# Reading two bands of the involution weights with one set of transfers, into two pair buffers of one tile

## The chip, the cores and the metric

The kernel runs on one core of one Trainium2 chip. The metric is the device time of one execution in microseconds; the median of three runs is the reference value. One further execution is taken with the hardware profiler, and every duration quoted below is from that one.

## What is computed

The input `x` is 32 images of 256 channels by 32 x 32 pixels in float32. Two layers follow each other, each with a group normalisation in front of it and a residual sum behind it. The first is a 3 x 3 convolution on values rounded to half precision, the second an involution: each pixel has its own 7 x 7 weights for each of 16 groups of channels, and these weights are made from the normalised image by two small matrix products.

```
x = x + conv3x3(quantize(gn(x))) + bias          # layer 0, 256 -> 256 channels
y = relu(bn(w1 @ gn(x)))                         # layer 1: 64 values for each pixel
w = w2 @ y + b2                                  # 16 groups x 49 taps for each pixel
out[g, c, h, w] = sum over 7x7 taps of w[g, tap, h, w] * gn(x)[g, c, h + dh, w + dw]
x = x + out
```

## The kernel before, in words

An image is cut in `K = 4` **bands** of 8 rows, and a band in a left and a right half of 16 columns. A half of a band is a **unit**: 8 units for each image (`M = 8`), 256 in all. Time is laid out by hand as **steps**, 16 for each image; the loop at the end walks through 570 steps and at each step issues, in this order, the next stage of up to four images' front, then the sums, the addition, the stores, the weights, the scatters, the loads of `x` and the loads of bands that are due. Every engine executes its own instructions in that order and waits on semaphores, which the recording layer derives from the tiles (named buffers) that an instruction reads and writes.

- **Front** (`front`, starting 56 steps ahead of an image's own first step): the statistics and the normalisation on ScalarE and VectorE, the convolution on TensorE (L332), the normalised image `xn`, the product `py` (L377) and `y_sb` (L388), and for each band the transposes `pt` (L396), which ScalarE copies into one of `NPIX = 6` `pixels` buffers (L400). The right half is stored mirrored (`backwards`).
- **Weights** (`weights`, 18 steps ahead, every second step): TensorE makes 4 rows of involution weights in `pw` (L411) and VectorE adds the bias and writes them into `w_sb`, a ring of `RING = 32` rows (`evict`, L435). `ring_pieces` cuts an eviction in pieces where the ring wraps.
- **Scatter** (`scatter`, L476): SyncE's queue issues seven transfers for each band that write `w_sb` into `wd`, a DRAM tensor in which every pixel holds its taps in the order in which they will be multiplied.
- **Band loads** (`load_bands`, L497, 9 steps ahead of a band's first step): for each of the 16 columns one transfer reads `wd` into a band buffer. There are `NBAND = 3` band buffers, each a tile of its own. A transfer has 8 rows by 2 halves, 16 runs of at most 4512 bytes. Two columns go to SyncE's queue, 14 to GpSimd's.
- **Sums** (`sums`, L522, one unit every second step): TensorE multiplies the `pixels` of the unit by its part of the band and accumulates in `acc`; one step later VectorE adds `acc` to the image in `x` (`add_windows`, L538), and `store` (L543) writes the image out in two halves.

Transfers issued on GpSimd's queue take eight completion semaphores in turn, so that each of them waits for the one that was issued eight before it.

Of the kernel before, what the change touches and what calls it, by code (L numbers as in the profile page):

```python
# [13 lines left out]
P = 128  # L14
# [22 lines left out]
XR = 4  # L37
# [22 lines left out]
TW = P // T  # L60
PAIR = 3 * GC
PAIRS = G // 2
ROW = S * WPIX
WR = 4
NBAND = 3
BY_SYNC = (0, 1)
ORDER = (0, 4, 8, 12, 2, 5, 9, 13, 3, 1, 6, 10, 14, 7, 11, 15)
NPIX = 6
RING = 32
SCRATCH = 4096  # L70
EARLY = CH + 4 + CH * CR
LATE = K1 * SW + 2 * 2 * SW
FRONT = -56
LOAD = -63
LEAD = 18


@with_exitstack
def tile_quant_conv_then_involution(
# [43 lines left out]
    x_tiles = {0: load_x(0)}  # L123


    ident = const.tile([P, P], F32, name="ident")
    make_identity(nc, ident)
    xq = const.tile([P, CH, H, W], F16, name="xq")
    eps = const.tile([P, 1], F32, name="eps")
# [13 lines left out]
    for t in bands[CH:]:  # L143
        nc.gpsimd.memset(t, 0.0)
    pixels = [const.tile([P, 2, PAIRS, PAIR], F32, name=f"pixels_{i}") for i in range(NPIX)]
    for t in pixels:
        nc.gpsimd.memset(t, 0.0)


    w_sb = const.tile([P, 2, RING, A, WIN, V], F32, name="w_sb")  # L150
    wd = dram.tile([H, S, WPIX], F32, name="wd")
    acc = [ps_acc.tile([P, RG, NT], F32, name=f"acc_{d}") for d in range(SIDES)]

    wq = const.tile([P, CH, K0 * K0, C], F16, name="wq")
    staged = []
    for kh in range(CH):
        wf = bands[kh].rearrange("p d n -> p (d n)")[:, : K0 * K0 * C].rearrange("p (k c) -> p k c", c=C)
# [21 lines left out]


    for col, cols, at, n in (
        (0, S, K1 * WB, PAD),
        (PAD1, PAD1, 0, PAD1 * WB),
        (W, PAD1, (K1 - PAD1) * WB, PAD1 * WB),
    ):
        to = bass.AP(
            tensor=wd.tensor,
            offset=wd.offset + col * WPIX + at,
            ap=[[ROW, H], [WPIX, cols], [1, n]],
        )  # L190
        nc.sync.dma_start(to, bands[NBAND - 1][:H, 0, :n].unsqueeze(1).to_broadcast([H, cols, n]))

    def quantize_weights(kh):

        nc.vector.tensor_scalar(wq[:, kh], staged[kh], F16_MAX, -F16_MAX, ALU.min, ALU.max)
        nc.gpsimd.memset(bands[kh], 0.0)
        if kh == CH - 1:
            nc.gpsimd.memset(w_sb, 0.0)

# [77 lines left out]
    def backwards(at):  # L277

        step, n = at.ap[-1]
        return bass.AP(tensor=at.tensor, offset=at.offset + step * (n - 1), ap=[*at.ap[:-1], [-step, n]])  # L280

    CONV = (9, 0, 9, 0)

    def front(b):
# [81 lines left out]
        for h in range(CH):  # L366
            yield
            to = xn[:, h].rearrange("p (k d r j) -> p d k r j", d=SIDES, r=TR, j=JC)
            at = xt[:, h].rearrange("p (k r d j) -> p d k r j", d=SIDES, r=TR, j=JC)
            gn.apply(h, [(to[:, 0], at[:, 0]), (to[:, 1], backwards(at[:, 1]))])  # L370
        yield from stages(2)

        py = ps_m.tile([P, NT], F32, tag="m", name="py")
# [10 lines left out]
        to = y_sb[b % 2].rearrange("p (k r d j) -> p d k r j", k=K, d=SIDES, j=JC)  # L384
        of = py.rearrange("p (k d r j) -> p d k r j", k=K, d=SIDES, j=JC)
        for d in range(SIDES):
            at = of[:, d]
            nc.scalar.activation(to[:, d], backwards(at) if d else at, AF.Relu, bias=bn_shift, scale=bn_scale)  # L388
        yield from stages(5)

        for m in range(0, M, 2):
            yield
            pt = ps_m.tile([P, 2, C], F32, tag="m", name="pt")
            for i in range(2):
                for h in range(CH):
                    nc.tensor.transpose(  # L396
                        pt[:, i, h * P : (h + 1) * P], xn[:, h, (m + i) * P : (m + i + 1) * P], ident
                    )
# [66 lines left out]
    def scatter(b, k, part):  # L465

        at = (b * H + k * TR) % RING
        for dj in range(part, K1, 2):
            t, e = divmod(dj, 2)
            to = bass.AP(  # L470
                tensor=wd.tensor,
                offset=wd.offset + k * TR * ROW + dj * WPIX + (K1 - 1 - dj) * WB,
                ap=[[WPIX, TW], [ROW, TR], [1, WB]],
            )
            rows = w_sb[t * TW : (t + 1) * TW, e, at : at + TR]
            nc.sync.dma_start(to, rows.rearrange("p s a r v -> p s (a r v)"))  # L476

    def load_bands(b, k):

        band = bands[(b * K + k) % NBAND]  # L480
        side = WINC * WB + PAD
        for i, j in enumerate(ORDER):
            cut = max(0, PAD1 - j)
            n = (K1 - cut) * WB + PAD
            src = bass.AP(
                tensor=wd.tensor,
                offset=wd.offset + k * TR * ROW + (j + PAD1) * WPIX + cut * WB,
                ap=[[ROW - V, TR], [(W - 1 - 2 * j) * WPIX - cut * WB, SIDES], [1, n]],
            )
            to = band[j::JC]  # L490
            to = bass.AP(
                tensor=to.tensor,
                offset=to.offset + (j + cut) * WB,
                ap=[to.ap[0], [side + (JC - 1 - 2 * j - cut) * WB, SIDES], [1, n]],
            )
            queue = nc.sync if j in BY_SYNC else nc.gpsimd
            queue.dma_start(to, src)  # L497

    def windows(b, m):
# [8 lines left out]
    def sums(b, m):  # L508

        k, d = divmod(m, SIDES)  # L510
        j0 = 0 if d else PAD1
        band = bands[(b * K + k) % NBAND][:, d]
        px = pixels[(b * K + k) % NPIX][:, d]
        for h in range(CH):
            for v in range(2):
                for g, at, top, f, l in windows(b, m):
                    p = slice(g * KP, (g + 1) * KP)
                    of = band[p, V * g * XR + j0 * WB : V * g * XR + (j0 + WINI) * WB]
                    of = of.rearrange("p (j a r v) -> p j a r v", a=A, r=WIN, v=V)
                    for t in range(T):  # L520
                        a = h * T + t
                        nc.tensor.matmul(  # L522
                            at[t * TW : (t + 1) * TW, h, :, f - top : l - top],
                            px[p, a, v * GC : v * GC + TW],
                            of[:, :, a, f - top : l - top, v],
                            start=(h, v) == (0, 0),
                            stop=(h, v) == (CH - 1, 1),
                        )
# [20 lines left out]
    def due(n, lag):  # L549

        b, i = divmod(n - lag, per)
        return (b, i) if 0 <= b < B else (None, None)

    with tc.manual_schedule():
        fronts = {}
        for n in range(FRONT, B * per + 2):
            b, i = due(n, FRONT)
            if i == 0:
                fronts[b] = front(b)
            later = list(fronts)  # L560
# [77 lines left out]
```

## Time and profile before

| what | value |
|---|---|
| runs | 1352.48 us median of 3 (1352.35 to 1356.02) |
| the profiled execution | 1344.24 us, of which 1342.5 us span |
| mean granted TensorE clock | 0.982 |
| TensorE busy | 1253.6 us, 93% of the span |
| GpSimd busy (band loads alone 980.3 us) | 1014.4 us, 76% |
| VectorE busy | 818.8 us, 61% |
| ScalarE busy | 733.3 us, 55% |
| DMA engines, mean busy share from 90 to 1200 us | 0.97 at 283 GB/s |
| band loads on GpSimd's queue | 1792, 549 ns each |
| band loads on SyncE's queue | 256 |
| scatters on SyncE's queue | 896, 160 KB each |

A page of the profile gives the busy time of each engine, the same in 40 slices of the span, the queues of the DMA engines, the chain of waits that ended last, and the costliest groups of instructions with what ended the idle time before them. PE is TensorE's matmul, PEld its weight load, DVE VectorE, ACT ScalarE, POOL GpSimd and SP SyncE; `L497` is line 497 of the kernel before. A row of the timeline has its start and its length in us, the engine, the line, what was written from what, how many, and in brackets the idle time ahead of it with what ended that. An average over the span mixes three stages: the start, in which only the front runs; a long steady stage; and the last three images, for which no front is left. A matmul of the kernel in float32 stands in the trace as two, so that a unit has 64 rows of L522 there.

### The profile page before, as it was taken

To read this page: it belongs to the slowest core of one execution; us is meant where nothing else is said; L and a number is where in the kernel's file an instruction comes from. 1 tells how busy PE (TensorE), PEld (TensorE's weight loads), DVE (VectorE), ACT (ScalarE), POOL (GpSimd) and SP (SyncE) were. 2 spreads that over 40 slices of the span, in tenths; PEclk is the share of its full clock that TensorE was granted. 3 is DMA by queue.
4 is the path that set the end of the run, shared out by engine and by line. 5 is a ranking of instruction groups with operands and counts; after the bars stand their busy time and mean duration, and the time that the engine had idled before them with its cause. 6 is when DMAs were issued, how large, how long until landed. Compare 5 with 4: busy or idle time off the path is not lost.

```text
span 1342.5 us, 65799 instructions
## 1 busy us (share of the span) xinstructions
PE 1253.6 (93%) x27648; PEld 763.7 (57%) x27648; DVE 818.8 (61%) x2539; ACT 733.3 (55%) x1731; POOL 1014.4 (76%) x1818
## 2 busy tenths in 40 slices
PE   5899999999999999999999999999999999999665
PEld 2356566565555655556655556666555566556454
DVE  3466666565666665656665666766666666666442
ACT  5775656455656556556545655655556564553300
POOL 9067878777787778777778787788777877788785
PEclk9999999999999999999999999999999999999987
DMA  6089999999999999999999999999999999999995
GB/s 228 11 237 295 271 293 293 279 266 281 272 286 282 291 285 270 283 263 280 293 282 283 270 288 282 293 297 296 281 288 275 277 284 290 271 281 266 278 274 166
DMA packets 360724, 361.85 MB, mean 270 GB/s; under 512 B 75056, under 2 KB 304752, under 8 KB 359152
## 3 DMA queue, kind: packets, MB, share of 16 engines
q1 hardware_dynamic: 278512, 229.38, 56.8%
q0 software_dynamic: 81920, 128.28, 33.9%
q8 instruction: 220, 3.60, 1.1%
q14 instruction: 72, 0.59, 0.1%
HBM read 176.60 MB, written 180.76 MB: 266 GB/s over the span
## 4 chain that ended last, share of the span: by engine, by line
PE 60%; DMA 23%; POOL 7%; issue 3%; ACT 3%; DVE 2%; SPq 1%; POOLq 0%; DVEq 0%; ACTq 0%
PE pc L332 25%; PE acc L522 19%; DMA band<-wd 17%; PE pw L411 11%; POOL band L497 7%; DMA wd<-w_sb 6%; PE pt L396 3%; PE py L377 3%; ACT junk L214 1%; SPq L476 1%; DVE w_sb L435 1%; DMA x<-in_x 1%; ACT xn L273 0%; SPq L497 0%; ACT xq L273 0%
## 5 line engine op out<-in xcount | busy, mean ns | idle before, releaser
L497 POOL DMA_DIRECT2D band<-wd x1792 | 980.3, 549 | 315.7 <-DMA band<-wd 182.0
L435 DVE TENSOR_TENSOR w_sb<-pw,late_sb 128x224 f32<-128x224 f32 (+7 forms) x1280 | 330.4, 322 | 419.5 <-PE pw L411 419.2
L332 PE MATMUL pc<-xq,wq 128*128 128x496 f16 (+3 forms) x2304 | 535.2, 379 | 20.3 <-ACT xq L273 18.3
L522 PE MATMUL acc<-band,pixels 64*32 64x190 f32 (+1 forms) x16384 | 426.6, 332 | 51.8 <-DMA band<-wd 42.7
L522 PEld LDWEIGHTS acc<-band,pixels 64*32 64x32 f32 x16384 | 304.7, 107 | 159.7 <-issue 81.1
L332 PEld LDWEIGHTS <-wq 128*128 128x128 f16 x2304 | 206.7, 98 | 316.1 <-issue 102.7
L411 PE MATMUL pw<-late_sb,y 64*32 64x224 f32 (+1 forms) x8192 | 288.9, 333 | 10.8 <-issue 9.4
L538 DVE TENSOR_TENSOR x<-acc,x 128x380 f32<-128x380 f32 (+1 forms) x512 | 262.0, 512 | 32.2 <-PE acc L522 23.2
L411 PEld LDWEIGHTS pw<-late_sb,y 64*32 64x32 f32 x8192 | 186.5, 106 | 38.1 <-issue 21.0
L400 ACT COPY pixels<-pt 128x512 f32<-128x512 f32 x128 | 73.7, 576 | 228.6 <-PE pt L396 228.6
L214 ACT ACTIVATE junk<-x 128x512 f16<-128x512 f32 (+1 forms) x192 | 146.4, 763 | 14.7 <-DVE x L348 12.2
L214 ACT ACTIVATE junk<-x,mean 128x1024 f16<-128x1024 f32 x128 | 147.1, 1149 | 4.3
L245 ACT ACTIVATE s<-back,eps 128x2 f32<-128x2 f32 x64 | 18.9, 296 | 178.6 <-DVE back L230 178.6
L346 DVE TENSOR_SCALAR q<-pc 128x512 f16<-128x512 f32 x128 | 87.2, 681 | 17.6 <-PE pc L332 17.6
L273 ACT ACTIVATE xn<-x,off,rstd 128x512 f32<-128x512 f32 x128 | 96.2, 800 | 0.0
L348 DVE SCALAR_TENSOR_TENSOR x<-q,early_sb,x 128x512 f32<-128x512 f16 x128 | 94.2, 736 | 0.3
L396 PEld LDWEIGHTS pt<-ident,xn 128*128 128x128 f32 x512 | 63.9, 142 | 26.3 <-issue 2.5
L396 PE MATMUL pt<-ident,xn 128*128 128x128 f32 x512 | 78.0, 275 | 0.1
L273 ACT ACTIVATE xq<-x,off,rstd 128x1024 f16<-128x1024 f32 x64 | 75.7, 1227 | 0.0
L235 ACT ACTIVATE mean<-back 128x2 f32<-128x2 f32 x64 | 12.6, 196 | 101.4 <-DVE back L230 101.4
L377 PE MATMUL py<-xn,early_sb 128*64 128x512 f32 x256 | 62.2, 606 | 0.9 <-ACT xn L273 0.9
L224 DVE STREAM_TRANSPOSE across<-sums 128x32 f32<-128x32 f32 x128 | 26.3, 205 | 33.6 <-ACT junk L214 32.4
(40 smaller groups left out, 369.3 us busy)
## 6 DMA issues: line engine op xcount, KB each, us to landing
wd<-w_sb SPq DMA_DIRECT2D x896, 160.0 KB
band<-wd POOLq DMA_DIRECT2D x1664, 70.5 KB, 4.6
x<-in_x SPq DMA_DIRECT2D x64, 512.0 KB
out<-x SPq DMA_DIRECT2D x64, 512.0 KB
band<-wd POOLq DMA_DIRECT2D x128, 60.5 KB, 4.6
band<-wd SPq DMA_DIRECT2D x128, 50.5 KB
band<-wd SPq DMA_DIRECT2D x128, 40.5 KB
band<-in_w SPq DMA_DIRECT2D x2, 1152.0 KB
```

Of the source, the lines that this page charges most:

```text
L214: nc.scalar.activation(junk[:, n0:n1], src[:, h, n0:n1], func, bias=bias, accum_out=self.sums[:, i : i + 1])
L273: nc.scalar.activation(dst, src, AF.Identity, bias=self.off[:, one], scale=self.rstd[:, one])
L332: nc.tensor.matmul(pc.rearrange("p (r c) -> p r c", c=W)[:, r0 - nt * RT : r1 - nt * RT, c0:c1], wq[:, kh, k, mh * P : (mh + 1) * P], xq[: ...
L346: nc.vector.tensor_scalar(q, pc, F16_MAX, -F16_MAX, ALU.min, ALU.max)
L348: nc.vector.scalar_tensor_tensor(xt[:, mh, cols], q, bias_sb[:, mh : mh + 1], xt[:, mh, cols], ALU.add, ALU.add)
L377: nc.tensor.matmul(py[i * CR : (i + 1) * CR], w1_sb[:, kh, :], px[:, :, i], start=kh == 0, stop=kh == CH - 1,)
L396: nc.tensor.transpose(pt[:, i, h * P : (h + 1) * P], xn[:, h, (m + i) * P : (m + i + 1) * P], ident)
L411: nc.tensor.matmul(pws[i][t * TW : (t + 1) * TW, : dj.stop - dj.start, r], y_sb[b % 2][half, (r0 // 2 + r) * W : (r0 // 2 + r + 1) * W], w ...
L435: nc.vector.tensor_tensor(to, of[:, :, d0:d1], bias[:, :, d0:d1], ALU.add)
L497: queue.dma_start(to, src)
L522: nc.tensor.matmul(at[t * TW : (t + 1) * TW, h, :, f - top : l - top], px[p, a, v * GC : v * GC + TW], of[:, :, a, f - top : l - top, v], ...
L538: nc.vector.tensor_tensor(x_at, of, x_at, ALU.add)
```

## The change

Bands 2q and 2q + 1 of an image become a **pair**, loaded together. `wd` is laid out so that the two bands of a pair lie beside each other along the columns (`SP = 2 * 32 + 6` columns, 8 rows for each of `K // BOTH = 2` pairs). A transfer of `load_bands` takes up to four halves of one column: 8 rows by 4 units, 32 runs. Ten columns (`d` is `None`) are read so, the six at the borders of the halves in two transfers of 16 runs each, one for the left halves and one for the right halves. A pair thus has 18 transfers on GpSimd's queue (`BY_GPSIMD`) and 4 on SyncE's (`BY_SYNC`).

The three band tiles are replaced by one tile `lot` of two `halves`, each of which holds a pair. In each half a hole between its second and third unit holds one of the `pixels` buffers; the hole of the first also holds the identity for the transposes. `NPIX` goes from 6 to 5, `RING` from 32 to 24, the scratch for descriptors from 4096 to 2048. The right half is no longer mirrored: `backwards` is gone. `LEAD` goes from 18 to 20, so weights and scatters come two steps earlier against the sums. The pixel copies of the third and fourth band of an image come 1 and 3 steps later (`HELD`). The band loads of a pair are issued 9 steps (GpSimd) and 8 steps (SyncE) ahead of its first sums; step 9 ahead comes right after the last sums that read the same half, and one step before the first sums of the pair in the other half.

```
-ROW = S * WPIX
+BOTH = 2
+SP = BOTH * W + 2 * PAD1
+ROW = SP * WPIX
+STEP = WINC * WB + PAD
+UNITS = BOTH * SIDES
+HALF = (UNITS - 1) * STEP + (JC + PAD1) * WB + PAD
+HOLE = (SIDES - 1) * STEP + JC * WB + PAD
+BY_SYNC = ((0, 0), (15, 1), (1, 0), (14, 1))
+BY_GPSIMD = (
+    (8, None), (4, None), (0, 1), (15, 0), (9, None), (5, None), (1, 1), (14, 0), (10, None),
+    (6, None), (2, 1), (13, 0), (11, None), (7, None), (2, 0), (13, 1), (12, None), (3, None),
+)
+NPIX = 5
+RING = 24
+SCRATCH = 2048
-NBAND = 3
-BY_SYNC = (0, 1)
-NPIX = 6
-RING = 32
-SCRATCH = 4096
-LEAD = 18
+LEAD = 20
+HELD = (0, 0, 1, 3)
...
+    lot = const.tile([P, 2 * HALF], F32, name="band_lot")
+    halves = [lot[:, i * HALF : (i + 1) * HALF] for i in range(2)]
+    holes = [t[:, HOLE : HOLE + 2 * PAD1 * WB] for t in halves]
+    ident = holes[0][:, 2 * PAIRS * PAIR :][:, :P]
...
-    bands = [const.tile([P, SIDES, WINC * WB + PAD], F32, name=f"band_{i}") for i in range(NBAND)]
...
-    wd = dram.tile([H, S, WPIX], F32, name="wd")
+    wd = dram.tile([K // BOTH, TR, SP, WPIX], F32, name="wd")
...
+            yield from stages(HELD[m // 2])
             to = pixels[(b * M + m) // 2 % NPIX].rearrange("p i a (v c) -> p (i a) v c", c=GC)
             nc.scalar.copy(to[:, :, ::2], pt.rearrange("p i (a v c) -> p (i a) v c", v=2, c=GC))
-            yield
+            yield from stages(1 - HELD[m // 2])
...
+    def load_bands(b, q, queue, columns):
+
+        for j, d in columns:
+            units, side, step = (UNITS, 0, 1) if d is None else (BOTH, d, SIDES)
+            cut = max(0, PAD1 - j) if d == 0 else 0
+            end = min(K1, JC + PAD1 - j) if d == 1 else K1
+            n = (end - cut) * WB + PAD
             src = bass.AP(
                 tensor=wd.tensor,
+                offset=wd.offset + (q * TR * SP + side * JC + j + PAD1) * WPIX + cut * WB,
+                ap=[[ROW - V, TR], [step * JC * WPIX, units], [1, n]],
             )
+            to = halves[(b * K // BOTH + q) % 2][j::JC]
...
-            b, i = due(n, 3 - 4 * NBAND)
-            if b is not None and i % 4 == 0:
-                load_bands(b, i // 4)
+            for lag, queue, columns in ((-9, nc.gpsimd, BY_GPSIMD), (-8, nc.sync, BY_SYNC)):
+                b, i = due(n, lag)
+                if b is not None and i % 8 == 0:
+                    load_bands(b, i // 8, queue, columns)
```

More of the change, by code (lines that the diff above doesn't have):

```diff
@@ L62 @@
 PAIRS = G // 2
-ROW = S * WPIX
-WR = 4
-NBAND = 3
-BY_SYNC = (0, 1)
-ORDER = (0, 4, 8, 12, 2, 5, 9, 13, 3, 1, 6, 10, 14, 7, 11, 15)
-NPIX = 6
-RING = 32
-SCRATCH = 4096
+BOTH = 2
[13 more added lines that the diff above has]
+SCRATCH = 2048
+WR = 4
 EARLY = CH + 4 + CH * CR
@@ L123, in tile_quant_conv_then_involution @@
     x_tiles = {0: load_x(0)}
-    ident = const.tile([P, P], F32, name="ident")
+    lot = const.tile([P, 2 * HALF], F32, name="band_lot")
+    halves = [lot[:, i * HALF : (i + 1) * HALF] for i in range(2)]
+    holes = [t[:, HOLE : HOLE + 2 * PAD1 * WB] for t in halves]
+    ident = holes[0][:, 2 * PAIRS * PAIR :][:, :P]
     make_identity(nc, ident)
@@ L141, in tile_quant_conv_then_involution @@
     y_sb = [const.tile([P, N // 2], F32, name=f"y_{i}") for i in range(2)]
-    bands = [const.tile([P, SIDES, WINC * WB + PAD], F32, name=f"band_{i}") for i in range(NBAND)]
-    for t in bands[CH:]:
+    parts = [halves[0][:, :HOLE], halves[0][:, HOLE + 2 * PAD1 * WB :]]
+    zeros = halves[1]
+    for t in (halves[1][:, :HOLE], halves[1][:, HOLE + 2 * PAD1 * WB :]):
         nc.gpsimd.memset(t, 0.0)
-    pixels = [const.tile([P, 2, PAIRS, PAIR], F32, name=f"pixels_{i}") for i in range(NPIX)]
+    pixels = [
+        t[:, : 2 * PAIRS * PAIR].rearrange("p (i a n) -> p i a n", i=2, n=PAIR) for t in holes
+    ]
+    pixels += [const.tile([P, 2, PAIRS, PAIR], F32, name=f"pixels_{i}") for i in range(2, NPIX)]
     for t in pixels:
@@ L156, in tile_quant_conv_then_involution @@
     for kh in range(CH):
-        wf = bands[kh].rearrange("p d n -> p (d n)")[:, : K0 * K0 * C].rearrange("p (k c) -> p k c", c=C)
+        wf = parts[kh][:, : K0 * K0 * C].rearrange("p (k c) -> p k c", c=C)
         nc.sync.dma_start(wf, w0[kh * P : (kh + 1) * P])
@@ L181, in tile_quant_conv_then_involution @@
     for col, cols, at, n in (
-        (0, S, K1 * WB, PAD),
+        (0, SP, K1 * WB, PAD),
         (PAD1, PAD1, 0, PAD1 * WB),
-        (W, PAD1, (K1 - PAD1) * WB, PAD1 * WB),
+        (BOTH * W, PAD1, (K1 - PAD1) * WB, PAD1 * WB),
     ):
@@ L188, in tile_quant_conv_then_involution @@
             offset=wd.offset + col * WPIX + at,
-            ap=[[ROW, H], [WPIX, cols], [1, n]],
+            ap=[[ROW, K // BOTH * TR], [WPIX, cols], [1, n]],
         )
-        nc.sync.dma_start(to, bands[NBAND - 1][:H, 0, :n].unsqueeze(1).to_broadcast([H, cols, n]))
+        nc.sync.dma_start(to, zeros[: K // BOTH * TR, :n].unsqueeze(1).to_broadcast([K // BOTH * TR, cols, n]))
     def quantize_weights(kh):
         nc.vector.tensor_scalar(wq[:, kh], staged[kh], F16_MAX, -F16_MAX, ALU.min, ALU.max)
-        nc.gpsimd.memset(bands[kh], 0.0)
+        nc.gpsimd.memset(parts[kh], 0.0)
         if kh == CH - 1:
@@ L275, in tile_quant_conv_then_involution @@
     LATER = 1
-    def backwards(at):
-        step, n = at.ap[-1]
-        return bass.AP(tensor=at.tensor, offset=at.offset + step * (n - 1), ap=[*at.ap[:-1], [-step, n]])
     CONV = (9, 0, 9, 0)
@@ L369, in front @@
             at = xt[:, h].rearrange("p (k r d j) -> p d k r j", d=SIDES, r=TR, j=JC)
-            gn.apply(h, [(to[:, 0], at[:, 0]), (to[:, 1], backwards(at[:, 1]))])
+            gn.apply(h, [(to[:, d], at[:, d]) for d in range(SIDES)])
         yield from stages(2)
@@ L386, in front @@
         for d in range(SIDES):
-            at = of[:, d]
-            nc.scalar.activation(to[:, d], backwards(at) if d else at, AF.Relu, bias=bn_shift, scale=bn_scale)
+            nc.scalar.activation(to[:, d], of[:, d], AF.Relu, bias=bn_shift, scale=bn_scale)
         yield from stages(5)
@@ L471, in scatter @@
                 tensor=wd.tensor,
-                offset=wd.offset + k * TR * ROW + dj * WPIX + (K1 - 1 - dj) * WB,
+                offset=wd.offset + (k // BOTH * TR * SP + k % BOTH * W + dj) * WPIX + (K1 - 1 - dj) * WB,
                 ap=[[WPIX, TW], [ROW, TR], [1, WB]],
@@ L476, in scatter @@
             nc.sync.dma_start(to, rows.rearrange("p s a r v -> p s (a r v)"))
[L478 to L484, printed above, removed]
+    def load_bands(b, q, queue, columns):
[4 more added lines that the diff above has]
+            n = (end - cut) * WB + PAD
             src = bass.AP(
                 tensor=wd.tensor,
-                offset=wd.offset + k * TR * ROW + (j + PAD1) * WPIX + cut * WB,
-                ap=[[ROW - V, TR], [(W - 1 - 2 * j) * WPIX - cut * WB, SIDES], [1, n]],
+                offset=wd.offset + (q * TR * SP + side * JC + j + PAD1) * WPIX + cut * WB,
+                ap=[[ROW - V, TR], [step * JC * WPIX, units], [1, n]],
             )
-            to = band[j::JC]
+            to = halves[(b * K // BOTH + q) % 2][j::JC]
             to = bass.AP(
                 tensor=to.tensor,
-                offset=to.offset + (j + cut) * WB,
-                ap=[to.ap[0], [side + (JC - 1 - 2 * j - cut) * WB, SIDES], [1, n]],
+                offset=to.offset + side * STEP + (j + cut - PAD1) * WB,
+                ap=[to.ap[0], [step * STEP, units], [1, n]],
             )
-            queue = nc.sync if j in BY_SYNC else nc.gpsimd
             queue.dma_start(to, src)
@@ L511, in sums @@
         j0 = 0 if d else PAD1
-        band = bands[(b * K + k) % NBAND][:, d]
+        band = halves[(b * K + k) // BOTH % 2]
+        unit = (k % BOTH * SIDES + d) * STEP - PAD1 * WB
         px = pixels[(b * K + k) % NPIX][:, d]
@@ L517, in sums @@
                     p = slice(g * KP, (g + 1) * KP)
-                    of = band[p, V * g * XR + j0 * WB : V * g * XR + (j0 + WINI) * WB]
+                    of = band[p, unit + V * g * XR + j0 * WB : unit + V * g * XR + (j0 + WINI) * WB]
                     of = of.rearrange("p (j a r v) -> p j a r v", a=A, r=WIN, v=V)
```

## The prediction

> **What bounds the kernel now.** I read the page first: its busy times, then its 40 slices.
>
> ```profile
> PE 1253.6 (93%) x27648; PEld 763.7 (57%) x27648; DVE 818.8 (61%) x2539; ACT 733.3 (55%) x1731; POOL 1014.4 (76%) x1818
> ...
> PE   5899999999999999999999999999999999999665
> ...
> POOL 9067878777787778777778787788777877788785
> ...
> DMA  6089999999999999999999999999999999999995
> ```
>
> TensorE is the bound for all but the ends: nine tenths or more in 35 slices, with the DMA engines just as full beside it. The waits say how little it lacks:
>
> ```profile
> PE acc L522 <- DMA band<-wd: 42.7, 22, 4.6
> ...
> POOL band L497 <- DMA band<-wd: 182.0, 237, 2.9
> ```
>
> Total, count and longest: the sums waited 42.7 us for bands in the whole run, 27.7 of it after 1200 us. So there is at most 3% to win. GpSimd's own 182 us are the eight semaphores taken in turn, and they are hidden. Next, one unit of the steady stage in the timeline (start, length):
>
> ```profile
> 620.01 1.59 PE L522 MATMUL acc<-band,pixels 64*32 64x190 f32 x64
> 621.40 0.95 PE L411 MATMUL pw<-late_sb,y 64*32 64x224 f32 x32
> 622.28 2.08 PE L332 MATMUL pc<-xq,wq 128*128 128x496 f16 x9
> 624.19 0.60 PE L396 MATMUL pt<-ident,xn 128*128 128x128 f32 x4
> ```
>
> TensorE takes its work strictly in this order. From 600 to 1000 us it executed 8831 of the 864 rows that an image has, 39.1 us for an image or **4.89 us for a unit**. Then the last band of the run and the start, where a load stands in the open:
>
> ```profile
> 1322.99 7.64 POOL L497 DMA_DIRECT2D band<-wd  x14 [0.21 <-issue]
> ...
> 1333.10 4.50 PE L522 MATMUL acc<-band,pixels 64*32 64x190 f32 x128 [2.76 <-DMA band<-wd]
> ```
>
> ```profile
> 64.44 9.11 SPq L476 DMA_DIRECT2D wd<-w_sb  x11
> 71.74 5.60 POOL L497 DMA_DIRECT2D band<-wd  x10 [37.12 <-DMA wd<-w_sb]
> ```
>
> 14 issues take 7.64 us, and the sums start 2.5 us after the last of them ends (1330.6 to 1333.1). A scatter issues at 0.83 us; seven from 64.44 end at 70.2, and the load waiting for them starts 1.5 us later.
>
> **The Trainium skill.** "DMA: Bandwidth & Descriptors", section "Anatomy of one DMA — SWDGE (gpsimd) path", puts a fixed part of about 2 us on each transfer, most of it the receipt of the last byte, and calls the descriptors' generation small. The 2.5 us above agrees; that generation stays small at 32 runs no row here shows. The same page, "Why a DMA increments its semaphore by 16 and not by 1", spreads a transfer over as many engines as the slowest dimension allows, which is 8 for 8 rows; the trace neither shows nor contradicts it. "TensorE: Matmul & The Clock Gate", Part 1 (the HAM clock gate), has TensorE at half clock after an idle window of about 3.4 us until it has been busy as long. The trace agrees in kind, even after a shorter gap:
>
> ```profile
> 1281.99 2.21 PE L522 MATMUL acc<-band,pixels 64*32 64x190 f32 x64 [2.06 <-DMA band<-wd]
> 1283.90 1.80 PE L411 MATMUL pw<-late_sb,y 64*32 64x224 f32 x32
> ...
> 1289.48 1.61 PE L522 MATMUL acc<-band,pixels 64*32 64x190 f32 x64
> 1290.84 1.00 PE L411 MATMUL pw<-late_sb,y 64*32 64x224 f32 x32
> ```
>
> The first unit after a wait costs 1.0 to 1.6 us more.
>
> **The change, part by part.**
>
> *Issue.* GpSimd has 18 transfers for a pair where it had 28: 1152 instead of 1792, 640 x 0.549 = 351 us less if a wide one costs no more. The bytes stay. Alone this gains only what the sums waited, at most 42.7 us.
>
> *The new wait.* Here the built program decides, its list of instructions with the semaphore values that each waits for. Before, the first sums of a band wait for that band's 14 transfers. After, the two halves lie in one tile, and the recording layer treats a load into one half as touching what the sums read in the other. The first sums of pair 0 wait for four of GpSimd's semaphores at 80 and four at 64: (4 x 80 + 4 x 64) / 16 = 36 transfers, **pair 0 and pair 1**. So it goes on: the sums of pair p wait for the loads of pair p + 1, issued one step before them. These in turn wait, rightly, for the last sums of pair p - 1, which read the same half. Two buffers thus work as one: a load starts when the last sums of a pair end, and the next sums start when it has landed. Behind TensorE's wait stand the convolution, weights and transposes of the next units, and so VectorE, ScalarE and the scatters.
>
> One cycle, from the first sums of a pair at 0 to those of the next:
>
> 1. The fourth unit's sums end at 3 x 4.89 + 1.59 = 16.3 us.
> 2. The second unit waits for the next pair's four loads on SyncE's queue, which wait for the first unit's sums: 1.6 + 4 x 0.594 (the median row of that queue's band loads) + 2.1 = 6.1, against 4.9 when TensorE gets there: +1.2.
> 3. Cold start after the long wait: +1.3, from the rows above. The sums end at 18.8.
> 4. The load: 8 transfers of 16 runs at 0.549 = 4.4. Ten of 32 runs: the row is silent on them. Transfers of 8 and of 16 runs both have 547 ns (the shortest and the median of L497), so the floor is 0.549; in proportion to runs it is 1.098. I take 0.62, near the floor, for the reason in the skill: 6.2. Landing and wake-up 2.5, with 0.5 for twice the bytes (an estimate: 33.9% of 16 engines' 1342.5 us over 1792 transfers is 4.06 engine-us each, over 8 engines 0.5), and 0.2 to see the release: 13.8.
> 5. For the second pair of an image the scatters are long done: 18.8 + 13.8 = **32.6 us**.
> 6. For its first pair they are not. The weights that complete its second band are made in the third unit (step 4 after the pair in front began), ending at 2 x 4.89 + 1.59 + 0.95 + 2.5 = 14.8; eviction 1.4 (a row of four takes 1.28), seven scatters 5.8, landing 1.5: 23.5. Then the load: **37.3 us**.
>
> That is 69.9 us for an image instead of 39.1. There are 62 such cycles, 31 of each kind: 2167 us.
>
> *Start.* Both pairs of image 0 must be in. The last weights for them come three units before the sums, which started at 87.7: near 79, and eviction to 80. SyncE's queue, still busy with band 2's scatters until 82.6, issues band 3's until 88.4; landing 1.5 and load 13.8 give the first sums at 104. *End.* In the last four loaded cycles the convolution is gone, 2.1 us for each of three or two units: -21. The last two pairs wait for nothing: 8 units at 1.6, 1.3 cold, and the 5 us from the last sums to the end: 19.
>
> Sum: 104 + 2167 - 21 + 19 = 2269 us of span, against 1342.5. The profiled execution lay 1.7 us above its span, and the median of the runs 0.6% above it: near **2280 us**.
>
> *Costed at nothing.* A ring of 24 rows is no multiple of 32, so evictions are cut oftener, 1920 pieces for 1280; a short one has 0.16 us, so VectorE gets 100 us more beside its 419 us of waiting for L411, and more now. The cut calls are never the one of step 6. `LEAD` 20 brings the scatters two steps earlier; counted in 6 and in the start. A pixel copy into a hole waits for all loads before it, by then demanded by the sums too: covered, and if not, ScalarE has over 600 us idle. Mirroring, `NPIX` and the scratch move no row on this path.
>
> **Rivals.**
>
> *The pairs are buffered as the step table means* (faster): the sums find their pair landed, because loads issued 9 steps, 22 us, ahead take 13.8. Then the 42.7 us go, less what a later start costs: 1310 us. For it: the waits above fit it well. Against: the listed values. It decides where the next pair lands inside the 3.3 us of weights and convolution between the last sums and the wait; 18 issues take 9.9 at their floor. 4%.
>
> *A wide transfer costs by its runs* (1.098): 10 x 0.48 x 62 = 298 more, 2575 us. For it: software writes these descriptors. Against: the equal 547 ns at 8 and 16 runs. 15%.
>
> *Quiet queues are quicker*: during a load nothing else moves, so landing 2.0 us, issue at the floor, no second wait and no cold start: (0.7 + 1.0 + 1.2 + 1.3) x 62 = 260 less, 2020 us. All at once 4%; part of it 10%.
>
> The serial cycle as priced has the rest, 67%.
>
> **How the numbers follow.** 2280 is the serial cycle. Step 4 unknown spans -0.7 to +4.8 us a cycle, steps 2 and 3 -2.5 to +1.5, the scatter 2 either way on half the cycles. Range 2110 to 2570, which leaves out the fast rival, half of the quiet one's extreme and the last of the dear one. A difference of 0.3% is about what a measurement of this kernel can tell from none: faster 4%, within it 1%, slower 95%.
>
> **What would show it.** Right: the sums wait for band loads about 62 times, alternately near 10 and near 15 us, some 800 us in all; TensorE's busy share near 57%; GpSimd idle until the fourth unit's sums end; a clock below 0.98. The wide issue's own row decides step 4. Wrong: waits of the sums under 50 us in all, or a second wait of each pair longer than its first.

## The result, and the profile after

The changed kernel takes 2401.8 us (median of four runs, 2401.5 to 2404.8) against 1353.9 us for the kernel before beside it: a ratio of 1.774, 95% interval 1.767 to 1.782. The forecast was 2280 us, range 2110 to 2570. The profiled execution has a span of 2399.8 us and a mean granted TensorE clock of 0.795 (0.982 before).

The page of the changed kernel, busy times and slices:

```profile
PE 1364.4 (57%) x27648; PEld 830.0 (35%) x27648; DVE 862.4 (36%) x3179; ACT 740.0 (31%) x1731; POOL 646.8 (27%) x1178
...
PE   5665565564564655654655655656646556556334
...
POOL 5322313313213223223123132132232232231231
...
DMA  2665665655665655665556656656556656665554
```

GpSimd's busy time went from 1014 to 647 us, as intended, and nothing else got shorter. TensorE and the DMA engines, nine tenths busy in nearly every slice before, are mostly at four to six. No engine is the bound; something waits in a ring. The waits, with total, count and longest, name its two sides:

```profile
PE acc L533 <- DMA band_lot<-wd: 995.1, 119, 19.1
```

```profile
SPq L507 <- PE acc L533: 1004.3, 63, 17.4
```

The sums wait 995 us for band loads (42.7 before), and SyncE's band loads wait 1004 us for sums. Of the 119 waits 63 are long, 927 us together; the 56 short ones have 1.2 us each. The first line alone would also fit slow loads. The second, with 63 entries for 64 pairs, says that the loads are not slow but late.

One turn of the ring, in three timelines (start, length, then in brackets the idle time in front and what ended it). TensorE:

```profile
1008.95 1.58 PE L533 MATMUL acc<-band_lot,pixels 64*32 64x190 f32 x64
1010.35 0.94 PE L422 MATMUL pw<-late_sb,y 64*32 64x224 f32 x32
1029.58 2.79 PE L533 MATMUL acc<-band_lot 64*32 64x190 f32 x64 [15.84 <-DMA band_lot<-wd]
1032.09 1.76 PE L422 MATMUL pw<-late_sb,y 64*32 64x224 f32 x32
...
1047.32 1.56 PE L533 MATMUL acc<-band_lot 64*32 64x190 f32 x63
```

GpSimd and SyncE:

```profile
1016.29 9.71 POOL L507 DMA_DIRECT2D band_lot<-wd  x18 [27.95 <-DMA wd<-w_sb]
1050.94 6.36 POOL L507 DMA_DIRECT2D band_lot<-wd  x12 [24.94 <-ACT rstd L282]
```

```profile
1001.23 11.61 SPq L487 DMA_DIRECT2D wd<-w_sb  x10
...
1035.21 7.61 SPq L487 DMA_DIRECT2D wd<-w_sb  x11
...
1043.38 3.00 SPq L487 DMA_DIRECT2D wd<-w_sb  x3
```

The last sums of a pair end at 1010.5; SyncE has issued the last scatter at 1012.8; GpSimd starts its 18 transfers at 1016.3, and 3.6 us after the last of them (1026.0) the next sums start. They end at 1048.9, and the next load starts at 1050.9. TensorE idles while a pair is loaded, GpSimd while it is multiplied. A bracket that names ScalarE's `rstd` is the last event before the start, not the cause: GpSimd reads nothing of it.

### The profile page after: what moved, and what is told of

Read it like the earlier page. It is cut to its first block, busy times and chain, and to the rows that moved or that the text cites. A ratio compares the mean times of both kernels' runs of the same rounds, so it can differ in the third digit from the quotient of the medians.

```text
span 2399.8 us, 65440 instructions
## 1 busy us (share of the span) xinstructions
PE 1364.4 (57%) x27648; PEld 830.0 (35%) x27648; DVE 862.4 (36%) x3179; ACT 740.0 (31%) x1731; POOL 646.8 (27%) x1178
## 4 chain that ended last, share of the span: by engine, by line
DMA 29%; PE 28%; POOL 19%; SPq 8%; DVE 6%; issue 5%; ACT 4%; POOLq 0%; DVEq 0%
DMA band_lot<-wd 21%; POOL band_lot L507 19%; PE acc L533 15%; DMA wd<-w_sb 8%; PE pc L343 6%; PE pw L422 5%; SPq L507 4%; SPq L487 4%; DVE w_sb L446 3%; ACT junk L230 1%; PE pt L406 1%; PE py L388 1%; DVE x L359 1%; ACT xn L289 1%; DVE x L549 1%
## 5 line engine op out<-in xcount | busy, mean ns | idle before, releaser
L507 POOL DMA_DIRECT2D band_lot<-wd x1152 | 612.1, 538 | 1725.1 <-DMA wd<-w_sb 565.2
L446 DVE TENSOR_TENSOR w_sb<-pw,late_sb 128x16 f32<-128x16 f32 (+9 forms) x1920 | 373.0, 263 | 1449.4 <-PE pw L422 1445.6
L533 PE MATMUL acc<-band_lot,pixels 64*32 64x190 f32 (+1 forms) x9728 | 292.3, 370 | 606.5 <-DMA band_lot<-wd 604.8
L533 PEld LDWEIGHTS acc<-band_lot,pixels 64*32 64x32 f32 x9728 | 204.7, 120 | 679.1 <-issue 641.1
L533 PE MATMUL acc<-band_lot 64*32 64x190 f32 (+1 forms) x6656 | 198.8, 369 | 390.3 <-DMA band_lot<-wd 390.3
L422 PE MATMUL pw<-late_sb,y 64*32 64x224 f32 (+1 forms) x8192 | 329.8, 369 | 5.9 <-ACT y L398 4.2
L533 PEld LDWEIGHTS acc<-band_lot 64*32 64x32 f32 x6656 | 139.8, 120 | 439.6 <-issue 415.7
L411 ACT COPY pixels<-pt 128x512 f32<-128x512 f32 x76 | 43.6, 573 | 415.1 <-PE pt L406 356.1
L406 PE MATMUL pt<-band_lot,xn 128*128 128x128 f32 x512 | 78.7, 277 | 2.2 <-ACT band_lot L411 2.1
L406 PEld LDWEIGHTS pt<-band_lot,xn 128*128 128x128 f32 x512 | 64.2, 143 | 28.9 <-ACT band_lot L411 3.5
## 6 DMA issues: line engine op xcount, KB each, us to landing
band_lot<-wd POOLq DMA_DIRECT2D x384, 70.5 KB, 3.3
```

The costliest lines, as they stand in the source:

```text
L406: nc.tensor.transpose(pt[:, i, h * P : (h + 1) * P], xn[:, h, (m + i) * P : (m + i + 1) * P], ident)
L422: nc.tensor.matmul(pws[i][t * TW : (t + 1) * TW, : dj.stop - dj.start, r], y_sb[b % 2][half, (r0 // 2 + r) * W : (r0 // 2 + r + 1) * W], w ...
L446: nc.vector.tensor_tensor(to, of[:, :, d0:d1], bias[:, :, d0:d1], ALU.add)
L533: nc.tensor.matmul(at[t * TW : (t + 1) * TW, h, :, f - top : l - top], px[p, a, v * GC : v * GC + TW], of[:, :, a, f - top : l - top, v], ...
```

## The experiments

The kernel before, run beside the others, had medians of 1350 to 1358 us. Cycles are measured in the timeline from the first sums of a pair to those of the next, and what is called an image is 16 steps, eight units; both are means over the steady part of a run. Experiments 2, 4, 6, 8 and 10 were run once, so a few us of theirs mean nothing.

**1. Two tiles.** Only the tile is split; addresses, order and transfers stay.

```diff
-    lot = const.tile([P, 2 * HALF], F32, name="band_lot")
-    halves = [lot[:, i * HALF : (i + 1) * HALF] for i in range(2)]
+    halves = [const.tile([P, HALF], F32, name=f"band_{i}") for i in range(2)]
```

> The changed kernel with its two halves as two tiles of their own; nothing else differs, and the sums of a pair then wait for that pair's loads alone. Serial theory (one tile makes the sums of a pair wait for the next pair's loads): the 995 us of waits for bands fall under 50 us and the time is 1300 to 1350 us. Rival A (the wide transfers, or two bands at a time, are what is late): the loads stay late and the time stays above 1900 us. Rival B (the rest of the change costs too: evictions cut oftener, pixel copies that wait for loads into their own half): some of it remains, 1370 to 1500 us.

Measured: 1668.4 us, ratio 1.232 (1.226 to 1.237). **733 of the 1048 us lost hang on these lines**: no instruction moved, only what the recording layer believes about two halves of one name. In the program that it builds, the first sums of pair 0 now wait for 18 of GpSimd's transfers and not for 36. But this is 310 us over the kernel before, so a second cost lay under the first. The waits of ScalarE and TensorE that show it:

```profile
ACT band L410 <- DMA wd<-w_sb: 207.7, 20, 17.3
```

```profile
PE pt L405 <- ACT band L410: 129.3, 18, 10.9
PE py L387 <- ACT band L410: 76.8, 12, 12.7
```

L410 is the pixel copy, and its target `band` is a hole in a half. By the program's semaphores these copies wait for the last load into that half (the scatter in the first line is only the last event). Of five images in a row two took 44 to 46 us and three 49 to 59, over and over: with `NPIX = 5` the hole slots fall on other bands in each image and are back after five.

**2. The kernel before, its three bands in one tile.**

```diff
-    bands = [const.tile([P, SIDES, WINC * WB + PAD], F32, name=f"band_{i}") for i in range(NBAND)]
+    lot = const.tile([P, NBAND, SIDES, WINC * WB + PAD], F32, name="band_lot")
+    bands = [lot[:, i] for i in range(NBAND)]
```

> The kernel before with its three band buffers laid in one tile, in the same places beside each other; nothing else differs. The first sums of a band then wait for the loads of the band two further, which wait for the sums just ended. Serial theory: one long wait for each band, a cycle of 6.5 us to the end of the second unit's sums, 1.3 for the cold start, 14 issues at 0.55 and 2.5 to land, 18.0 us, 126 times, with 104 before and 20 after: near 2390 us, 2250 to 2600. Rival A: no pair, no wide transfer, no cut ring, so nothing is late and the time stays at 1354 us.

Measured: 2687.3 us. The one tile ruins the other kernel too, with its narrow transfers, three buffers and no holes: the sums wait 1195 us in 126 waits, one for each band. The cycle is 20.4 us where I expected 18.0, so the mechanism held and its size was missed.

**3. The kernel before with a shorter ring.**

```diff
-RING = 32
+RING = 24
```

> The kernel before with a ring of 24 rows in place of 32 and nothing else, so 1920 pieces of eviction for 1280. The prediction's costing at nothing: within 0.3% of before, VectorE busy some 40 to 100 us more. Rival B: the longer evictions hold up the next weights and scatters on TensorE's path, 5 to 30 us slower.

Measured: 1356.5 us, ratio 0.9999 (0.9978 to 1.0021). VectorE has 862.0 us instead of 818.8, and TensorE's busy time stays at 1253.6. The 640 extra pieces are free.

**4. The changed kernel with one half in use**, its loads listed one step ahead.

```diff
-            to = halves[(b * K // BOTH + q) % 2][j::JC]
+            to = halves[0][j::JC]
...
-        band = halves[(b * K + k) // BOTH % 2]
+        band = halves[0]
...
-            for lag, queue, columns in ((-9, nc.gpsimd, BY_GPSIMD), (-8, nc.sync, BY_SYNC)):
+            for lag, queue, columns in ((-1, nc.gpsimd, BY_GPSIMD), (-1, nc.sync, BY_SYNC)):
```

> The changed kernel using one half of its tile only: every pair is loaded into the first half, right after the last sums that read it, and summed from there. The scatters then come eight steps ahead of the load that reads them. Serial theory (the two halves already work as one, and late scatters lengthen its cycle): all 63 cycles cost 16.3 us of units, 2 cold and 13.4 of load, 31.7 us, without the short second wait: near 2110 us, faster than the 2402 us with two halves. Rival (the second half hides part of the load): slower than 2402 us by what it hid.

Measured: 2251.1 us with **half the buffer**, 151 us faster than the changed kernel. In one tile the second half was worth less than nothing. The edit does two things, and the 151 us are not divided between them: with one half the second wait of each pair is gone (68 us in all in the changed kernel), and loads that are listed later start 0.5 to 0.8 us after the last sums, no longer held up by scatters. Cycles are 33.6 and 35.1 us and not as short as expected: the scatters, which overwrite the part of `wd` that a load reads, now wait for loads, which they did not in the changed kernel.

```profile
SPq L487 <- DMA band_lot<-wd: 587.2, 152, 11.1
```

**5. Two tiles, and nothing written inside a half.** On top of experiment 1, all pixel buffers are tiles of their own; constants take their place in the holes.

```diff
-    pixels = [
-        t[:, : 2 * PAIRS * PAIR].rearrange("p (i a n) -> p i a n", i=2, n=PAIR) for t in holes
-    ]
-    pixels += [const.tile([P, 2, PAIRS, PAIR], F32, name=f"pixels_{i}") for i in range(2, NPIX)]
+    pixels = [const.tile([P, 2, PAIRS, PAIR], F32, name=f"pixels_{i}") for i in range(NPIX)]
...
-    y_sb = [const.tile([P, N // 2], F32, name=f"y_{i}") for i in range(2)]
+    y_sb = [const.tile([P, N // 2], F32, name="y_0")] * 2
...
```

> The changed kernel with each half in a tile of its own, and nothing that is written during the run left inside a half: all five pixel buffers are tiles of their own. The room comes from constants (identity, w1, w2 and the biases of the convolution), which lie in the two holes instead and are only read, and from one y buffer in place of two. In the run with two tiles alone (1668.4 us) TensorE still lost about 345 us to waits, and ScalarE 208 + 45 us in 24 pixel copies into the holes, which wait for the last load into the same half. Theory (these copies are the second cost, everything else runs beside the matmuls): 310 us go, 1310 to 1390 us, and no wait of over 5 us behind a pixel copy is left. Rival (the second cost is the burst itself: 18 wide transfers that meet the stores and scatters on the DMA engines, the copies only wait with it): 1550 to 1670 us, with TensorE waiting at the sums for the loads instead of at the transposes.

Measured: 1532.2 us, ratio 1.135 (1.131 to 1.139). Neither of the two. The copies' waits are gone, and every image takes 44 to 48 us, what only the two good ones of five took before; so **the holes cost some 136 us** (130 by the two ratios). The edit also takes one y buffer away, but no wait for it shows in the profile. I had put all 310 us on the holes, and 180 remain. TensorE and GpSimd wait so:

```profile
PE acc L530 <- DMA wd<-w_sb: 99.9, 33, 7.9
PE acc L530 <- DMA band<-wd: 30.3, 6, 11.4
```

```profile
POOL band L504 <- DMA wd<-w_sb: 318.4, 27, 47.9
```

The sums read no scatter. SyncE's loads and scatters are counted on the same semaphores, so the first line too is a wait for loads.

**6. The same with one tile again.**

```diff
-    halves = [const.tile([P, HALF], F32, name=f"band_{i}") for i in range(2)]
+    lot = const.tile([P, 2 * HALF], F32, name="band_lot")
+    halves = [lot[:, i * HALF : (i + 1) * HALF] for i in range(2)]
```

> The same kernel as the one with own pixel buffers, but with the two halves in one tile again. Theory (the one tile alone makes the cycle of sums, load, sums; while it stands, pixel copies in the holes are covered by it): no gain against the changed kernel, 2370 to 2430 us, cycles of 37 and 35.5 us as there. Rival (the holes cost their 310 us in any arrangement, and the two costs add up): about 2090 us.

Measured: 2397.3 us, cycles of 37.2 and 35.5 us. While the one tile stands, the holes cost nothing: the costs do not add up, the larger hides the smaller.

**7. The kernel before with the small edits together.**

```diff
-NPIX = 6
-RING = 32
-LEAD = 18
+NPIX = 5
+RING = 24
+LEAD = 20
+HELD = (0, 0, 1, 3)
...
+            yield from stages(HELD[m // 2])
...
-            yield
+            yield from stages(1 - HELD[m // 2])
```

> The kernel before with the small edits of the change together and without the wide transfers: ring of 24 rows, five pixel buffers, weights 20 steps ahead in place of 18, pixel copies held back by 0, 0, 1 and 3 stages. My theory costs all of these at nothing: within 0.5% of the kernel before, 1347 to 1361 us. Rival (the later pixel copies come too near to the sums that read them, or ScalarE's order changes): 1% or more slower, with new waits of TensorE for the pixels.

Measured: 1366.6 us, ratio 1.011 (1.007 to 1.016), just past what I allowed and with the rival's sign. The new wait is not for pixels at the sums but at `py`:

```profile
PE py L378 <- ACT pixels L402: 22.5, 27, 1.8
```

The held copy of an image's fourth band comes one step before the `py` of the next image, which needs the same PSUM buffer. In the kernel before, `py` waited 0.9 us in all, for `xn`. That this wait makes the 16 us is likely and not shown: the first sums also start 6.5 us later (94.2 instead of 87.7), and of the four edits only the ring was run alone.

**8. The changed kernel, its loads reading another DRAM array.**

```diff
+    other = dram.tile([K // BOTH, TR, SP, WPIX], F32, name="other")
...
-                tensor=wd.tensor,
+                tensor=other.tensor,
```

> The changed kernel (one tile), but the loads of the bands read another scratch array in DRAM, filled with zeros once, so that no load waits for a scatter; scatters still run, and the sums are of zeros. Left out: the weights in the sums. Theory (the second pair of an image took 35.5 instead of 32.6 us because the scatters, bunched behind the stall, end late for it too; the first pair took 37.4 for the same reason): load starts 2.0 us after the last sums in both, lasts 9.7 us and lands 3.3 later, the sums' cycle without the wait is 18.3, so both cycles take about 33.3 us and the run about 2210 us (2170 to 2260), even and odd within 1 us of each other. Rival (the load's own length or the wait for ScalarE, not the scatters, sets both): about 2400 us, even and odd still about 2 us apart.

Measured: 2238.0 us; cycles of 33.2 and 34.2 us instead of 37.4 and 35.5. The late scatters cost 4.2 us in the cycle from an image's first pair to its second, but only 1.3 in the one from the second. A cycle from a second pair, with the last sums and then the load:

```profile
1999.69 0.91 PE L536 MATMUL acc<-band_lot 64*32 64x133 f32 x30
```

```profile
2001.22 7.40 POOL L510 DMA_DIRECT2D band_lot<-other  x14 [23.55 <-ACT t L275]
2009.34 2.26 POOL L510 DMA_DIRECT2D band_lot<-other  x4 [0.72 <-DMA band_lot<-other]
```

The load starts 0.6 us after the last sums, not 2.0 as I expected, its issues take 10.4 us, not 9.7, and the sums in front of it are longer: errors that cancel in the 33.3 us. The two kinds of cycle differ by 1.0 us, the edge of what I had allowed. (The sums multiply zeros, which may move the clock a little, as shorter waits may: 0.817 against 0.795.)

**9. Experiment 5, SyncE's four loads of a pair moved to the end of GpSimd's eighteen.**

```diff
-            for lag, queue, columns in ((-9, nc.gpsimd, BY_GPSIMD), (-8, nc.sync, BY_SYNC)):
+            for lag, queue, columns in ((-9, nc.gpsimd, BY_GPSIMD + BY_SYNC),):
```

> The kernel with two tiles and own pixel buffers (1532 us), with the four loads of a pair that SyncE issued moved to the end of GpSimd's eighteen. There SyncE's queue stood before these loads for 203 us, waiting for the scatters it had itself just issued to land (about 4 to 5 us for each of 62 pairs), with the next scatters queued behind it, and an image took 45.5 us against some 40 in the kernel before. Theory (SyncE's queue, with its waits, is what an image's 45.5 us are): an image gets back to 40 to 42 us, 1345 to 1430 us in all, for 2.2 us more of issue per pair on GpSimd, which has time. Rival (a pair can only be loaded when the scatters of its second unit have landed, one or two steps before the load is listed, whoever issues it, so the load is late anyway): 1500 to 1560 us, with TensorE still waiting at the first sums of a pair for about 3 us.

Measured: 1585.5 us, ratio 1.174 (1.169 to 1.178): my theory fell, and the result is 25 us past the rival's range. An image takes 47.3 us instead of 45.7. GpSimd still waits for the scatters (417 us instead of 318), and the four issues more come at the end of a load that is late already:

```profile
PE acc L530 <- DMA band<-wd: 116.7, 25, 10.1
```

**10. Experiment 5 with the loads of experiment 8.**

```diff
-                tensor=wd.tensor,
+                tensor=other.tensor,
```

> The kernel with two tiles and own pixel buffers (1532 us), its loads reading another scratch array that is filled with zeros once, so that they wait for no scatter. Left out: the weights in the sums. Both theories on the lateness of the scatters (SyncE's own wait, or the pair that needs its second unit's scatters) expect the loads to be in time: 1340 to 1400 us. Rival (the burst of eighteen wide transfers, or the transfers' meeting on the DMA engines, holds it up by itself): 1480 to 1540 us.

Measured: 1399.4 us. The same eighteen wide transfers in a burst, but waiting for no scatter, and the sums hardly wait for loads:

```profile
PE acc L533 <- DMA band<-other: 8.9, 2, 4.5
```

```profile
POOL band L507 <- PE acc L533: 480.8, 58, 45.0
```

GpSimd's loads now wait for the one thing they should, the last sums of the same half. An image takes 41.0 us (39.8 in the kernel before). The first sums start at 116.9 us instead of 99.3, since the other array has to be filled first, so some 150 of experiment 5's 180 us are the wait for scatters. The edit would also free scatters from waiting for loads, but in experiment 5 none of them did.

**11 and 12. Experiment 5, with three of each band's seven scatters issued by GpSimd, or by ScalarE.**

```diff
-            nc.sync.dma_start(to, rows.rearrange("p s a r v -> p s (a r v)"))
+            queue = nc.gpsimd if part else nc.sync
+            queue.dma_start(to, rows.rearrange("p s a r v -> p s (a r v)"))
```

> The kernel with two tiles and own pixel buffers (1532 us), with the second part of each unit's scatters (3 of 7, so 12 of 28 an image) issued by GpSimd instead of SyncE. With loads that wait for no scatter the same kernel took 1399 us, so some 133 us are the loads' wait for the scatters of the pair's second unit; a scatter takes about 1 us of SyncE's queue, so three fewer bring a unit's last landing about 3 us forward, as much as TensorE waits at the first sums of a pair. Theory (the end of the second unit's scatters sets when a load starts): 1410 to 1490 us. Rival (GpSimd's queue holds scatters and loads in one order, its scatters wait behind loads that wait for a half, and those loads behind scatters): no gain or a loss, 1530 to 1620 us.

```diff
+            queue = nc.scalar if part else nc.sync
```

> The same three of seven scatters of a unit issued by ScalarE, which is idle half of the time (742 of 1530 us busy) and issues no load. Theory (scatters end about 3 us earlier): 1410 to 1490 us. Rival (each issue stands in ScalarE's order before its own work, 12 of them an image with a wait for the evictions; that delays normalisation and pixel copies as much as it helps the loads): 1500 to 1620 us, with TensorE waiting for ScalarE at the transposes, py or the convolution.

Measured: 1587.2 us (ratio 1.169, 1.160 to 1.178) and 1566.0 us (1.153, 1.146 to 1.159). Both rivals were right. By GpSimd, its scatters stand behind loads, so SyncE's loads wait longer for them, 378 us instead of 203, and VectorE's evictions wait 298 us for room in the ring instead of 147. By ScalarE, the pixel copies stand behind scatters, and TensorE behind the copies, 94 us where it was 20:

```profile
SPq L505 <- DMA wd<-w_sb: 378.2, 47, 13.7
```

```profile
PE py L385 <- ACT pixels L408: 94.0, 30, 7.1
```

**The account**, each line from its own run:

| kernel | us | image, us | what this line adds |
|---|---|---|---|
| before | 1353.9 | 39.8 | |
| 7: before, small edits | 1366.6 | 40.2 | the small edits together: 16, against 1350.4 beside it |
| 10: two tiles, own pixels, no scatter waited for | 1399.4 | 41.0 | 18 are the filling of the other array; 15 not assigned |
| 5: two tiles, own pixels | 1532.2 | 45.7 | a pair waits for its scatters: 133, with the filling 151 |
| 1: two tiles | 1668.4 | 44 to 59 | writes into the holes wait for loads: 136 |
| after: one tile | 2401.8 | 72.9 | loads of the other half are waited for: 733 |

No version here beats the kernel before, and none of the runs points to one: experiment 10, without the wait for scatters and less its 18 us of filling, is still at 1382. It is open why the scatters of a pair's second band can't be had earlier. For the first pair of an image they are listed two and one steps ahead of the load that needs them, in the kernel before three to six, and three ways of relieving SyncE's queue each lost 34 to 55 us. Earlier weights would need an earlier front, and with it a second `xn`, for which there was no room; that was not tried.

## Why the prediction was right, point by point

*The new wait.* Right, and shown: experiment 1 takes it away by naming, 2 puts it into the other kernel, 4 shows that the second half bought nothing. Of the signs I had named, the sums waited alternately near 13 and near 16 us (forecast 10 and 15), 927 us in all (800), and TensorE's busy share is 57%, as forecast. Experiments 6 and 8 leave the ring in place and change what lies on it or not, as its steps say.

*Issue.* 368 us less on GpSimd against 351 forecast, worth nothing. A wide transfer has a median of 534 ns (534 to 682), so the rival of cost by runs is out, and my 0.62 was too much by 0.09. I had also misread the row of the kernel before: 547 ns is the figure of its transfers of 16 runs, and those of 8 runs have 551.

*Steps 1 to 3.* The sums of a pair were to end 18.8 us after its first; in the cycle shown it is 19.3, on average 18.6 for an image's first pair and 19.4 for its second. The second wait is 1.2 us as forecast; the cold start is 2.0 (2.79 and 1.76 us against 1.58 and 0.94) where 1.3 stood. The Trainium skill's "TensorE: Matmul & The Clock Gate", Part 1, has half clock after a wait of this length; the first unit's times are 1.8 and 1.9 fold, and the granted clock over its 2.79 us is 0.50, which agrees.

*Step 4.* 13.8 us forecast; in the cycles shown 13.3 and 14.2. The first is made up otherwise than I had it: 9.7 of issue instead of 10.6, and 3.6 from the last issue to the sums instead of 3.0. In the second the issues take 11.2, since GpSimd waits between them for its own earlier transfers:

```profile
1058.30 0.54 POOL L507 DMA_DIRECT2D band_lot<-wd  x1 [1.00 <-DMA band_lot<-wd]
```

*Step 5 is the one that failed*: "the scatters are long done". The cycle from a second pair takes 35.5 us instead of 32.6. I had the scatters of a second pair run ahead as before, though I had written that they stand behind TensorE's wait. By the prices of step 6 they would land at 18.6 us of that cycle (9.9 for the weights in its second unit, 1.4, 5.8 and 1.5), which is only just before its sums end; and the seven of the pair's first band are issued ahead of them. In the timeline after 1029.6 all the scatters come bunched, 14 of them until 1046.4, and the load starts 2.1 us after the last sums instead of 0.2.

How much this costs, experiment 8 shows: without scatters to wait for, this cycle takes 34.2 us, so **the scatters are 1.3 of the 2.9 us**. The other 1.6 are small misses of steps 1 to 4 in this pair: on average its sums end at 19.4 us, its issues take 11.0, and the sums follow them after 3.4 (forecast 18.8, 10.6 and 3.0). Over 31 cycles the 2.9 us make 90 us, 40 of them by the scatters.

*Step 6.* 37.3 forecast, 37.4 measured, the mechanism right and the figure partly luck: on average the load starts at 24.2 us of the cycle and not at 23.5, and from there to the sums it takes 13.2 and not 13.8.

*Start and end.* The first sums came at 115.9 instead of 104 (12 us). The 21 us off for the missing convolution did not come: the last four loaded cycles take 36.2, 35.1, 37.2 and 34.1 us, 3 us less than four others; why the convolution's work was worth so little there was not tried. From the first sums of the last two pairs to the end it is 24 us, not 19. Together with the cycles from second pairs (90) and from first pairs (3): 12 + 90 + 3 + 18 + 5 = 128 of the 131 us by which the span exceeds my 2269.

*Costed at nothing.* The ring: right (experiment 3; VectorE has 44 us more, not 100). The pixel copies in the holes: "covered" is right (experiment 6), but "if not, ScalarE has over 600 us idle" is wrong. Idle time in total is no cover for a wait in the middle of an ordered queue: 136 us. The held copies: not named. On the kernel before the small edits cost 16 us together, with a new wait of 22.5 us for these copies; in the changed one that wait is 2.2.

*The fast rival* would not have come true without the one tile either. It took the loads to start 9 steps ahead; they start when the scatters have landed. Its 1310 us stand against 1532 in experiment 5.

## What to carry to other kernels

Before two buffers are cut from one named tile, look in the built program at what the first reader of one waits for: here that alone made 733 us of a change whose transfers became cheaper just as intended. Joining transfers joins their preconditions too: a pair is ready when its slower member is, and what fills it may need a longer lead, though no run here had one. And when one large wait is removed, the work it covered has to be priced again from nothing; three costs lay under each other here.

## What the runs showed of the hardware

- The issue of a transfer by GpSimd hardly depends on its runs. Medians in the kernel before: 551 ns for 8 runs of 9.0 KB, 547 for 16 of 4.5 KB. In the changed kernel: 532 to 553 for 16 runs, by the column, and 534 for 32. A scatter of 256 runs of 640 bytes has 583 (experiment 11).
- Landing went more by company than by size: the 141 KB transfers have a median of 3.7 us and the 70.5 KB ones 3.3 in the half-idle changed kernel; in experiment 5 they have 5.4 and 5.1, and in the kernel before the 70.5 KB ones 4.6.
- In the changed kernel TensorE's granted clock fell to 0.795, a mean over the span with its waits, and the same 27648 instructions were busy for 1364 instead of 1254 us. The kernels that wait less lie between: 0.951 and 1297 us in experiment 5, 0.977 and 1262 in experiment 10 (on zeros).
- The traces record that clock in windows of 3.41 us, each at full or at half clock, and how busy TensorE was in one window goes with the clock of the next. In the kernel before, the 10 full-clock windows that half clock followed had TensorE busy for at most 0.44 of them, the 357 that full clock followed for at least 0.50. In the changed kernel the two meet at 0.42 to 0.43 (67 and 330 windows), and none of the 68 half-clock windows that full clock followed was busy for less than 0.76. So a single wait of under 3 us can be enough: one of 2.65 us in the kernel before left TensorE busy for 1.12 of the 3.40 us up to 586.4, and the next 3.40 us had a clock of 0.50. A few windows of experiments 7, 9 and 11 do not fit: half clock followed shares of up to 0.56.
